# A graph layer's own-row messages: from one per row tile, closed by an identity product, to one per four tiles, transposed, added to the copied sums

## The chip, the cores and the metric

The kernel runs on one core of one Trainium2 chip. The metric is the device time of one execution in microseconds. The core has five engines that run their own instruction queues in order: TensorE (PE; its weight loads are listed as PEld), VectorE (DVE), ScalarE (ACT), GpSimd (POOL) and SyncE (SP, which here issues the transfers). They wait for each other through semaphores.

## The reference, cut to what matters

Four graph layers follow each other on 2708 rows of 128 features. The adjacency matrix `adj` is 2708 by 2708, symmetric in its pattern, with under one per cent of its entries set and every diagonal entry set. The change is in layer 1:

```python
h = maximum(layernorm(x), 0)
s = h @ msg_w[:, :D].T
d = h @ msg_w[:, D:].T
messages = gelu(s[:, None, :] + d[None, :, :] + msg_b)
aggregated = einsum('ijd,ij->id', messages, adj)
new = concatenate([h, aggregated], -1) @ upd_w.T + upd_b
x = x + layernorm(gelu(new) + h)
```

Row i receives, from every column j with adj[i, j] not zero, a message weighted by that entry. One of these columns is j = i: the message of the row to itself is gelu(h_i @ (W_s + W_d) + msg_b), weighted by adj[i, i]. That one message per row is what the change treats differently.

## The kernel before, in words

Layer 0 (to about 215 us) reads the adjacency matrix once, forms layer 0's product with it, writes a transposed copy, and lists for each row, in 22 blocks of 124 columns, up to eight entries per block (`val`, `col`). The diagonal entries are taken out of these lists and kept in `own`, a tile of 128 partitions by 22 row tiles (L292 fills it).

Layer 1 (about 215 to 615 us) works on 22 row tiles of 128 rows (the last has 20). A prologue (L827 to L839) enters layer 0's result, normalises, transposes h into `hT`, and forms the split destination rows `d3` (three bf16 parts). Then comes one period for each row tile, `period(t)`, L709, with steps k = 0 to 5. The order of all instructions on every engine is that of this hand-written sequence: the whole stretch stands under a manual schedule (L826). In one period:

- `combine(t, k)` (L602) adds, by one-hot bf16 products on TensorE, source and destination rows of four blocks into the PSUM tile `p_m`, which has two buffers; `activate(t, k)` (L621) takes the Gelu on ScalarE into `g`.
- `gather(t, k)` (L627), two steps later, multiplies `g` with `put` (the weights at their rows) in fp32 and adds into `agg`, the transposed sums, one PSUM tile for four row tiles.
- `put` for the next tile is written partly by GpSimd (`put_values`, L530, eight instructions at the start of a period) and partly by ScalarE (`put_more`, L540).
- For later tiles, at the same time: `pass_on` (L548), `fetch` (L485), `rank` (L459), `describe` (L465), `select_rows` (L472), `columns` (L562), `place` (L499), `finish_rows` (L481). The last four are VectorE's. The product of `fetch` reads the tile `sel` that `finish_rows` wrote at step 4 of the period before.
- Every even period calls `sources(k)` (L570) at step 2 for the next pair of tiles: a product with 256 columns (L580: 128 for the source part, 128 for the sum of both weight halves, `src_self`), one VectorE addition out of PSUM (L587), the split of the source half into three bf16 parts (`split`, L416), and for the other half a Gelu (L596) and two scalings by `own` (L599) on ScalarE. The result `gs` is the weighted message of each row to itself.
- `close_tile(t - 1)` (L639) at step 1 adds `gs` to the sums through a product with the identity (L645), and after the last tile of a group of four copies the sums to SBUF (`aggT`, L649 to L654).
- `update(g, step)` (L660) works on a finished group in eight steps over eight periods. Step 0 falls into period 4g+5: the product `p_u` (L671, L672), which reads `aggT`.

PSUM tiles with the tag "r" share one buffer (the pool of L405 has one): `p_r` of `rank`, `p_w` of `pass_on`, `p_s` of `sources` and `p_u` of `update` are written one after the other, each after the last reader of the one before.

Layers 2 and 3 (from about 615 us) begin with transfers of the transposed matrix (`a<-adjT`, L1082), which write memory that layer 1 has used; their first one waits for the last product of layer 1 (L672).

Of the kernel before, what the change touches and what calls it, by code (L numbers as in the profile page):

```python
# [20 lines left out]
F32 = mybir.dt.float32  # L21
BF16 = mybir.dt.bfloat16
AF = mybir.ActivationFunctionType
# [7 lines left out]
P = 128  # L31
N = 2708
D = 128
# [27 lines left out]
def listed_layers(ctx: ExitStack, tc: tile.TileContext, x, adj, w, out, flag):  # L61
# [85 lines left out]
    def span(t, k):  # L147

        return t * P, min(k * P, N - t * P)
# [245 lines left out]
    with (  # L395
# [11 lines left out]
        msg_wT, upd_wT = load(fix, "msg_wT"), load(fix, "upd_wT")  # L407
        upd_b, ln_w, ln_b = load_rows(fix, "upd_b"), load_rows(fix, "ln_w"), load_rows(fix, "ln_b")
        msg_b = load_rows(fix, "msg_b")

        src_self = fix.tile([P, 2, D], F32, name="src_self")
        nc.vector.tensor_copy(src_self[:, 0, :], msg_wT[:, 0, :])
        nc.vector.tensor_tensor(src_self[:, 1, :], msg_wT[:, 0, :], msg_wT[:, 1, :], ALU.add)

        d3 = fix.tile([P, NB, 3, D], BF16, name="d3")
        def split(dst, src, rest):  # L416

            nc.scalar.copy(dst[0], src)
            nc.vector.tensor_tensor(rest, src, dst[0], ALU.subtract)
            nc.scalar.copy(dst[1], rest)  # L420
            nc.gpsimd.tensor_tensor(dst[2], rest, dst[1], ALU.subtract)
# [145 lines left out]

        own_rows, aggs = {}, {}

        def sources(k):  # L570

            p = rpool.tile([P, CH], F32, tag="r", name="p_s")
            pv = p.rearrange("p (t c d) -> p t c d", t=2, c=2)
            sb = once.tile([P, 2, 2, D], F32, name="sb")
            m = size(2 * k + 1)
            if m < P:
                nc.vector.memset(sb[:, 1, :, :], 0.0)
            for q in range(2):
                c, mq = (2 * k + q) * P, size(2 * k + q)
                nc.tensor.matmul(  # L580
                    p[0:mq, q * 2 * D : (q + 1) * 2 * D], hT[:, c : c + mq],
                    src_self.rearrange("p c d -> p (c d)"), start=True, stop=True,
                )
            bv = msg_b.unsqueeze(1).to_broadcast([P, 2, D])
            if m == P:
                bv = msg_b.unsqueeze(1).unsqueeze(1).to_broadcast([P, 2, 2, D])
                nc.vector.tensor_tensor(sb, pv, bv, ALU.add)  # L587
            else:
                for q in range(2):
                    mq = size(2 * k + q)  # L590
                    nc.vector.tensor_tensor(sb[0:mq, q, :, :], pv[0:mq, q, :, :], bv[0:mq, :, :], ALU.add)
            s3 = three.tile([P, 3, 2, D], BF16, name="s3")
            rest = once.tile([P, 2, D], F32, name="s_r")
            split([s3[:, q, :, :] for q in range(3)], sb[:, :, 0, :], rest)
            gs = three.tile([P, 2, D], F32, name="gs")
            nc.scalar.activation(gs, sb[:, :, 1, :], AF.Gelu)  # L596
            for q in range(2):
                t = 2 * k + q
                nc.scalar.activation(gs[:, q, :], gs[:, q, :], AF.Identity, scale=own[:, t : t + 1])  # L599
            own_rows[k] = s3, gs  # L600

        def combine(t, k):  # L602

            st = state[t]
            s3 = own_rows[t // 2][0]
            b0 = 4 * k
            n = min(4, NB - b0)
            p = mpool.tile([P, 4, D], F32, name="p_m")
            for b in range(b0, b0 + n):
                kb = width(b)  # L610
                for q in range(3):
                    nc.tensor.matmul(  # L612
                        p[:, b - b0, :], st["sel"][:, b, :], s3[:, q, t % 2, :], start=(q == 0), stop=False
                    )
                for q in range(3):
                    nc.tensor.matmul(  # L616
                        p[:, b - b0, :], st["cols"][0:kb, b, :], d3[0:kb, b, q, :], start=False, stop=(q == 2)
                    )
            st["p", k] = p
# [7 lines left out]
        def gather(t, k):  # L627

            st = state[t]
            m = size(t)  # L630
            if k == 0 and t % 4 == 0:
                aggs[t // 4] = acc.tile([P, 4, P], F32, name="agg1")
            agg = aggs[t // 4][:, t % 4, 0:m]
            g = st.pop(("g", k))
            for b in range(4 * k, min(4 * k + 4, NB)):
                put = (st["put", 0][:, b, 0:m] if b < HP else st["put", 1][:, b - HP, 0:m])
                nc.tensor.matmul(agg, g[:, b - 4 * k, :], put, start=(b == 0), stop=False)  # L637

        def close_tile(t):  # L639

            state.pop(t)
            m = size(t)
            g = t // 4
            gs = own_rows[t // 2][1]
            nc.tensor.matmul(aggs[g][:, t % 4, 0:m], gs[0:m, t % 2, :], ident[0:m, 0:m], start=False, stop=True)  # L645
            first, k = GROUPS[g]
            if t == first + k - 1:
                p = aggs[g]
                aggs[g] = once.tile([D, 4, P], F32, name="aggT")  # L649
                if m < P:  # L650
                    nc.scalar.copy(aggs[g][:, 0 : k - 1, :], p[:, 0 : k - 1, :])
                    nc.scalar.copy(aggs[g][:, k - 1, 0:m], p[:, k - 1, 0:m])
                else:
                    nc.scalar.copy(aggs[g][:, 0:k, :], p[:, 0:k, :])  # L654


        STEPS = 8
# [51 lines left out]
        def period(t, between=()):  # L709
# [5 lines left out]
            for k in range(GB):  # L715
# [17 lines left out]
                    fetch(t + 2, k - 1)  # L733
                if k == 1 and a:
                    describe(t + 3)
                if k == 2:
                    if now and t % 2 == 0 and t + 2 < NT:
                        sources(t // 2 + 1)
                    if a:
                        select_rows(t + 3)  # L740
                    if now and t + 4 < NT:
                        count_rows(t + 4)
                    updates(t)
# [64 lines left out]

        def split_destinations(g):

            rest = once.tile([P, 4, D], F32, tag="sb", name="d_r")
            for src, dst, q0, q1, k in state.pop(("d", g)):
                r = rest[0:k, q0:q1, :]
                nc.vector.tensor_tensor(r, src, dst[0], ALU.subtract)
                nc.scalar.copy(dst[1], r)
                nc.gpsimd.tensor_tensor(dst[2], r, dst[1], ALU.subtract)
# [9 lines left out]
        with tc.manual_schedule():  # L826
            for step, n in (  # L827
# [877 lines left out]
```

## Time and profile before

| | |
|---|---|
| median of three runs | 1073.51 us (1072.81 to 1073.60) |
| span of the profiled execution (first to last instruction) | 1069.6 us |
| outside that span, taken against the median | 3.9 us |
| layer 1's loop, 280 to 615 us: PE, DVE, ACT, POOL busy | 323.7, 249.6, 214.7, 208.2 us of 335 |
| layer 1's prologue, 215 to 280 us: PE, DVE, ACT, POOL busy | 30.0, 47.8, 28.4, 20.9 us of 65 |
| granted TensorE clock in the prologue and in the loop | 0.62 and 1.00 |

The profile lists no separate total time for the profiled execution; its span of 1069.6 us is what the working below is made against, and the rest of 3.9 us is taken as unchanged. A row of the profile's groups reads: line, engine, operation, output<-input, shape, count, busy time in us, mean ns of one, then the idle time just before it and what ended that. A matmul in fp32 is listed as two records. Durations of matmuls overlap (they are pipelined), so what one costs is read from the distance of starts, not from its duration.

### The profile page before, as it was taken

How to read it: one execution, taken by the hardware profiler on the slowest of the kernel's cores; microseconds unless marked ns; L12 is line 12 of the kernel's file. 1: busy time of each engine (PE TensorE's matmuls, PEld its weight loads, DVE VectorE, ACT ScalarE, POOL GpSimd, SP SyncE). 2: the span in 40 equal slices, each digit the busy share in tenths (PEclk: the TensorE clock that was granted, in tenths of full speed). 3: DMA queues.
4: the chain of work that ended last, by engine and by line, in shares of the span. 5: the costliest groups of instructions: out<-in, count | busy, mean ns of one | idle time of the engine just before them, and what ended most of it. 6: DMA issues, size and time to landing. Idle time of an engine off the chain costs nothing. (4 is left out here: it accounts for less than half of the span.)

```text
span 1069.6 us, 21992 instructions
## 1 busy us (share of the span) xinstructions
PE 950.0 (89%) x7950; PEld 754.1 (71%) x7950; DVE 824.4 (77%) x2853; ACT 515.4 (48%) x1428; POOL 398.7 (37%) x476
## 2 busy tenths in 40 slices
PE   5798889934799999999999979999978999999993
PEld 2454445433799999899899934444578999999772
DVE  7999999768577798787878265666578977997673
ACT  7777777634766666666666522433321200320142
POOL 3311112022776656666766163343410300430132
PEclk9999999766799999999999979999989999999996
DMA  9888996221233433322221075566300000000000
GB/s 365 315 303 316 316 342 243 78 65 46 88 109 106 124 95 106 106 91 83 97 96 57 28 256 186 185 225 216 91 22 26 9 1 1 6 15 1 2 15 14
DMA packets 60625, 129.67 MB, mean 121 GB/s; under 512 B 11160, under 2 KB 23828, under 8 KB 57798
## 3 DMA queue, kind: packets, MB, share of 16 engines
q1 hardware_dynamic: 58690, 125.38, 34.2%
q10 hardware_dynamic: 1816, 2.80, 0.8%
q8 instruction: 64, 1.05, 0.4%
q14 instruction: 55, 0.45, 0.1%
HBM read 81.55 MB, written 30.87 MB: 105 GB/s over the span
## 5 line engine op out<-in xcount | busy, mean ns | idle before, releaser
L955 PE MATMUL att<-hv,wt 128*128 128x129 f32 (+2 forms) x1936 | 243.8, 283 | 8.7 <-DVE wt L923 8.7
L955 PEld LDWEIGHTS att<-hv,wt 128*128 128x128 f32 (+2 forms) x1936 | 224.7, 192 | 25.8 <-DVE wt L923 10.1
L923 DVE SCALAR_TENSOR_TENSOR wt<-row,lift,mask 128x1024 f32<-128x1024 f32 (+5 forms) x176 | 160.3, 939 | 34.9 <-PE att L955 34.8
L536 POOL TENSOR_SCALAR put<-mine,value 128x128 f32<-128x128 bf16 x176 | 149.8, 867 | 70.3 <-DVE mine L433 67.9
L612 PE MATMUL p_m<-s,sel 128*128 128x128 bf16 x1452 | 161.6, 220 | 5.4 <-ACT g L624 5.4
L616 PE MATMUL p_m<-d,cols 124*128 124x128 bf16 (+1 forms) x1452 | 161.7, 220 | 1.4 <-DVE cols L566 1.3
L121 POOL TENSOR_TENSOR n_r<-n_r,minus_half 128x4 f32<-128x4 f32 (+1 forms) x31 | 46.1, 1486 | 286.5 <-DVE n_r L120 280.9
L637 PE MATMUL agg<-put,g 128*128 128x128 f32 (+1 forms) x968 | 135.9, 281 | 0.0
L297 PE MATMUL acc<-a,hs 128*128 128x512 f32 (+2 forms) x264 | 124.4, 574 | 10.8 <-ACT hs L137 10.8
L309 PEld LDWEIGHTS p_T<-ident,a 128*128 128x128 f32 x484 | 60.1, 144 | 88.3 <-issue 40.3
L637 PEld LDWEIGHTS agg<-put,g 128*128 128x128 f32 x968 | 118.2, 192 | 0.0
L1094 PE MATMUL p_agg<-a,hs 128*128 128x512 f32 (+2 forms) x264 | 109.3, 556 | 7.3 <-DMA a<-adjT 7.2
L612 PEld LDWEIGHTS <-sel 128*128 128x128 bf16 x1452 | 104.3, 98 | 10.8 <-issue 7.0
L285 DVE FIND_INDEX8 col<-val,a 128x8 uint16<-128x124 f32 (+1 forms) x400 | 108.1, 285 | 0.0
L309 PE MATMUL p_T<-ident,a 128*128 128x128 f32 x484 | 82.3, 289 | 26.2 <-ACT aT L313 19.4
L624 ACT ACTIVATE g<-p_m 128x512 f32<-128x512 f32 x132 | 73.1, 554 | 63.8 <-PE p_m L616 63.8
L616 PEld LDWEIGHTS <-cols 124*128 124x128 bf16 (+1 forms) x1452 | 102.5, 98 | 1.9 <-DVE cols L566 1.9
L544 ACT ACTIVATE put<-mine,value 128x128 f32<-128x128 bf16 x308 | 100.5, 391 | 0.0
L283 DVE MAX8 val<-a 128x8 f32<-128x124 f32 (+1 forms) x400 | 92.8, 276 | 2.5 <-DMA a<-in_adj 2.5
L313 ACT ACTIVATE aT<-p_T 128x512 f32<-128x512 f32 (+2 forms) x132 | 71.1, 541 | 47.9 <-ACT aT L313 32.7
L1094 PEld LDWEIGHTS p_agg<-a,hs 128*128 128x128 f32 (+1 forms) x264 | 47.5, 194 | 55.8 <-issue 54.2
L297 PEld LDWEIGHTS acc<-a,hs 128*128 128x128 f32 (+1 forms) x264 | 44.7, 202 | 25.9 <-issue 14.8
(252 smaller groups left out, 1418.7 us busy)
## 6 DMA issues: line engine op xcount, KB each, us to landing
a<-in_adj SPq DMA_DIRECT2D x21, 1354.0 KB
adjT<-aT SPq DMA_DIRECT2D x105, 256.0 KB
a<-adjT SPq DMA_DIRECT2D x20, 1280.0 KB
spread<-passed SPq DMA_DIRECT2D x22, 704.0 KB
later<-sel SPq DMA_DIRECT2D x22, 616.0 KB
row<-own_d ACTq DMA_DIRECT2D x10, 256.0 KB
later<-sel SPq DMA_DIRECT2D x22, 82.5 KB
adjT<-aT SPq DMA_DIRECT2D x21, 74.0 KB
```

Source lines behind the costliest of these rows:

```text
L283: nc.vector.max(val[:, n, b, :], block(b))
L285: nc.vector.max_index(col[:, n, b, :], val[:, n, b, :], block(b))
L297: nc.tensor.matmul(accs[ci][:, 0:cw], h[0:m, n, :], sets[n // 4][0:m, n % 4, c : c + cw], start=(n == 0), stop=(n == NT - 1),)
L309: nc.tensor.transpose(p[0:k, q * P : q * P + m], sets[gi][0:m, q, j * P : j * P + k], ident[0:m, 0:m])
L536: nc.gpsimd.tensor_scalar(st["put", 0][:, b, :], st["mine"][:, b, :], st["value"][:, b : b + 1], None, ALU.mult)
L544: nc.scalar.activation(st["put", 1][:, b - HP, :], st["mine"][:, b, :], AF.Identity, scale=st["value"][:, b : b + 1])
L612: nc.tensor.matmul(p[:, b - b0, :], st["sel"][:, b, :], s3[:, q, t % 2, :], start=(q == 0), stop=False)
L616: nc.tensor.matmul(p[:, b - b0, :], st["cols"][0:kb, b, :], d3[0:kb, b, q, :], start=False, stop=(q == 2))
L637: nc.tensor.matmul(agg, g[:, b - 4 * k, :], put, start=(b == 0), stop=False)
L923: nc.vector.scalar_tensor_tensor(wt[0:kj, :], row[0:kj, k, c : c + n], lift[0:kj, j, k : k + 1], mask[0:kj, j, c : c + n], op0=ALU.max, op ...
L955: nc.tensor.matmul(banks[s // 3][0:m, s % 3, :], wt[0:kj, q * P : q * P + m], hv[0:kj, j, k, :], start=(v < 2 and s // 3 not in touched), ...
L1094: nc.tensor.matmul(pa[:, 0:n], h[0:k, j, :], a[0:k, j - j0, 0:n], start=(j == 0), stop=(j == NT - 1))
```

## The change

`sources` no longer forms the own message: its product has 128 columns, the VectorE addition 256 elements, and the Gelu and the two scalings are gone. In their place, for each group of four row tiles:

- `self_messages(g)`, step 2 of period 4g+1: one product of `w_self` (the sum of the weight halves) with 512 columns of `hT`, into a new PSUM tile `p_self` of the tag "r"; a Gelu with the bias column `msg_b1` on ScalarE into `gs`, transposed and with one buffer.
- `load_own(g)`, step 2 of period 4g: a transfer that spreads the group's diagonal entries to all partitions (`own_b`). They come from `own_dram`, written in the prologue by `turn_own` (a transposition on TensorE, a ScalarE copy, a transfer).
- `weigh_selfs(g)`, last step of period 4g+1: GpSimd multiplies `gs` by `own_b`.
- In `close_tile`, after the copy to `aggT`, GpSimd adds `gs` to it; the identity product is gone.

`w_self` is formed by GpSimd; VectorE's two instructions for `src_self` are gone. `split_destinations` keeps its scratch under another tag.

```diff
@@ layer 1, weights
+        msg_b1 = fix.tile([P, 1], F32, name="msg_b1")
+        nc.sync.dma_start(msg_b1, w["msg_b"].rearrange("(k p) -> p k", p=P), allow_slow_non_contiguous=True)
-        src_self = fix.tile([P, 2, D], F32, name="src_self")
-        nc.vector.tensor_copy(src_self[:, 0, :], msg_wT[:, 0, :])
-        nc.vector.tensor_tensor(src_self[:, 1, :], msg_wT[:, 0, :], msg_wT[:, 1, :], ALU.add)
+        w_self = fix.tile([P, D], F32, name="w_self")
+        nc.gpsimd.tensor_tensor(w_self, msg_wT[:, 0, :], msg_wT[:, 1, :], ALU.add)
@@ new functions
+        own_dram = dram.tile([NT, P], F32, name="own_dram")
+        def turn_own(_):
+            p = rpool.tile([P, CH], F32, tag="r", name="p_own")
+            nc.tensor.transpose(p[0:NT, 0:P], own, ident)
+            turned = once.tile([NT, P], F32, name="own_T1")
+            nc.scalar.copy(turned, p[0:NT, 0:P])
+            nc.sync.dma_start(own_dram, turned)
+        def load_own(g):
+            t, k = GROUPS[g]
+            n = span(t, k)[1]
+            own_cols[g] = once.tile([P, CH], F32, name="own_b")
+            nc.sync.dma_start(
+                own_cols[g][:, 0:n],
+                own_dram[t : t + k, :].rearrange("t i -> (t i)")[0:n].partition_broadcast(P),
+            )
+        def self_messages(g):
+            c, n = span(*GROUPS[g])
+            p = rpool.tile([P, CH], F32, tag="r", name="p_self")
+            nc.tensor.matmul(p[:, 0:n], w_self, hT[:, c : c + n], start=True, stop=True)
+            selfs[g] = once.tile([D, CH], F32, name="gs")
+            nc.scalar.activation(selfs[g][:, 0:n], p[:, 0:n], AF.Gelu, bias=msg_b1)
+        def weigh_selfs(g):
+            n = span(*GROUPS[g])[1]
+            nc.gpsimd.tensor_tensor(selfs[g][:, 0:n], selfs[g][:, 0:n], own_cols.pop(g)[:, 0:n], ALU.mult)
@@ sources
-            sb = once.tile([P, 2, 2, D], F32, name="sb")
+            sb = once.tile([P, 2, D], F32, name="sb")
-                nc.tensor.matmul(
-                    p[0:mq, q * 2 * D : (q + 1) * 2 * D], hT[:, c : c + mq],
-                    src_self.rearrange("p c d -> p (c d)"), start=True, stop=True,
-                )
+                nc.tensor.matmul(pv[0:mq, q, :], hT[:, c : c + mq], msg_wT[:, 0, :], start=True, stop=True)
-                nc.vector.tensor_tensor(sb, pv, bv, ALU.add)
+                nc.vector.tensor_tensor(sb, pv, msg_b.unsqueeze(1).to_broadcast([P, 2, D]), ALU.add)
-            gs = three.tile([P, 2, D], F32, name="gs")
-            nc.scalar.activation(gs, sb[:, :, 1, :], AF.Gelu)
-            for q in range(2):
-                t = 2 * k + q
-                nc.scalar.activation(gs[:, q, :], gs[:, q, :], AF.Identity, scale=own[:, t : t + 1])
@@ gather, close_tile
-                nc.tensor.matmul(agg, g[:, b - 4 * k, :], put, start=(b == 0), stop=False)
+                nc.tensor.matmul(agg, g[:, b - 4 * k, :], put, start=(b == 0), stop=(b == NB - 1))
-            nc.tensor.matmul(aggs[g][:, t % 4, 0:m], gs[0:m, t % 2, :], ident[0:m, 0:m], start=False, stop=True)
+                n = span(first, k)[1]
+                flat = aggs[g].rearrange("d t i -> d (t i)")[:, 0:n]
+                nc.gpsimd.tensor_tensor(flat, flat, selfs.pop(g)[:, 0:n], ALU.add)
@@ period
+                if k == 2 and now and t % 4 == 1:
+                    self_messages(t // 4)
+                if k == GB - 1 and now and t % 4 == 1:
+                    weigh_selfs(t // 4)
+                if k == 2 and now and t % 4 == 0:
+                    load_own(t // 4)
                 if k == 2:
                     if now and t % 2 == 0 and t + 2 < NT:
                         sources(t // 2 + 1)
@@ split_destinations
-            rest = once.tile([P, 4, D], F32, tag="sb", name="d_r")
+            rest = once.tile([P, 4, D], F32, tag="aggT", name="d_r")
@@ prologue
-                (place, 0), (pass_on, 0), (sources, 0), (enter, 3), (spread_sums, 4), (split_destinations, 1),
+                (place, 0), (pass_on, 0), (turn_own, 0), (sources, 0), (enter, 3), (spread_sums, 4), (split_destinations, 1),
```

More of the change, by code (lines that the diff above doesn't have):

```diff
@@ L570, in sources @@
+        own_cols, selfs = {}, {}
         def sources(k):
             p = rpool.tile([P, CH], F32, tag="r", name="p_s")
-            pv = p.rearrange("p (t c d) -> p t c d", t=2, c=2)
-            sb = once.tile([P, 2, 2, D], F32, name="sb")
+            pv = p[:, 0 : 2 * D].rearrange("p (t d) -> p t d", t=2)
+            sb = once.tile([P, 2, D], F32, name="sb")
             m = size(2 * k + 1)
             if m < P:
-                nc.vector.memset(sb[:, 1, :, :], 0.0)
+                nc.vector.memset(sb[:, 1, :], 0.0)
@@ L578, in sources @@
             for q in range(2):
                 c, mq = (2 * k + q) * P, size(2 * k + q)
-                nc.tensor.matmul(
-                    p[0:mq, q * 2 * D : (q + 1) * 2 * D], hT[:, c : c + mq],
-                    src_self.rearrange("p c d -> p (c d)"), start=True, stop=True,
-                )
-            bv = msg_b.unsqueeze(1).to_broadcast([P, 2, D])
+                nc.tensor.matmul(pv[0:mq, q, :], hT[:, c : c + mq], msg_wT[:, 0, :], start=True, stop=True)
             if m == P:
-                bv = msg_b.unsqueeze(1).unsqueeze(1).to_broadcast([P, 2, 2, D])
-                nc.vector.tensor_tensor(sb, pv, bv, ALU.add)
+                nc.vector.tensor_tensor(sb, pv, msg_b.unsqueeze(1).to_broadcast([P, 2, D]), ALU.add)
@@ L590, in sources @@
                     mq = size(2 * k + q)
-                    nc.vector.tensor_tensor(sb[0:mq, q, :, :], pv[0:mq, q, :, :], bv[0:mq, :, :], ALU.add)
+                    nc.vector.tensor_tensor(sb[0:mq, q, :], pv[0:mq, q, :], msg_b[0:mq, :], ALU.add)
             s3 = three.tile([P, 3, 2, D], BF16, name="s3")
             rest = once.tile([P, 2, D], F32, name="s_r")
-            split([s3[:, q, :, :] for q in range(3)], sb[:, :, 0, :], rest)
-            gs = three.tile([P, 2, D], F32, name="gs")
-            nc.scalar.activation(gs, sb[:, :, 1, :], AF.Gelu)
-            for q in range(2):
-                t = 2 * k + q
-                nc.scalar.activation(gs[:, q, :], gs[:, q, :], AF.Identity, scale=own[:, t : t + 1])
-            own_rows[k] = s3, gs
+            split([s3[:, q, :, :] for q in range(3)], sb, rest)
+            own_rows[k] = s3
         def combine(t, k):
             st = state[t]
-            s3 = own_rows[t // 2][0]
+            s3 = own_rows[t // 2]
             b0 = 4 * k
@@ L643, in close_tile @@
             g = t // 4
-            gs = own_rows[t // 2][1]
-            nc.tensor.matmul(aggs[g][:, t % 4, 0:m], gs[0:m, t % 2, :], ident[0:m, 0:m], start=False, stop=True)
             first, k = GROUPS[g]
```

## The prediction

> **What bounds the kernel now.** First the page: busy shares and slices.
>
> ```profile
> PE 950.0 (89%) x7950; PEld 754.1 (71%) x7950; DVE 824.4 (77%) x2853; ACT 515.4 (48%) x1428; POOL 398.7 (37%) x476
> ...
> PE   5798889934799999999999979999978999999993
> ...
> PEclk9999999766799999999999979999989999999996
> ```
>
> TensorE is the fullest engine; in layer 1's loop (slices 11 to 22, 280 to 615 us) it is at 90% or more. So I asked what ends its idle time there, 285 to 600 us:
>
> ```profile
> PE p_m L612 <- ACT g L624: 5.4, 7, 1.4
> PE y L493 <- DVE sel L483: 3.0, 4, 0.9
> PE p_m L616 <- DVE cols L566: 1.3, 2, 0.6
> ```
>
> Only 9.7 us: work taken from TensorE's queue moves the loop's end, except where ScalarE or VectorE comes last. The seven ScalarE waits all lie in even periods, those with `sources`. ScalarE in period 12:
>
> ```profile
> 467.76 0.41 ACT L420 CAST s<-s_r 128x256 bf16<-128x256 f32 x1 [0.49 <-DVE s_r L419]
> 468.08 0.41 ACT L596 ACTIVATE gs<-sb 128x256 f32<-128x256 f32 x1
> 468.52 0.69 ACT L599 ACTIVATE gs<-gs,own 128x128 f32<-128x128 f32 x2
> 469.12 1.63 ACT L137 ACTIVATE hs<-xs,n_r 128x128 f32<-128x128 f32 x4
> 470.66 0.97 ACT L544 ACTIVATE put<-mine,value 128x128 f32<-128x128 bf16 x3
> 471.53 0.57 ACT L624 ACTIVATE g<-p_m 128x512 f32<-128x512 f32 x1
> ```
>
> From here ScalarE runs without a gap until the Gelu whose end releases TensorE at 472.16 (wait 1.45). The two `gs` rows, 468.08 to 469.12, are 1.04 us of that chain, and the change removes them. Third, TensorE at step 2 of period 9, where the new product will stand:
>
> ```profile
> 416.94 1.11 PE L637 MATMUL agg<-put,g 128*128 128x128 f32 x8
> 417.89 0.44 PE L493 MATMUL y<-xb,sel 128*128 128x37 bf16 x11
> 418.17 0.47 PE L671 MATMUL p_u<-upd_wT,hT 128*128 128x128 f32 x2
> ```
>
> Starts matter, not durations: eight fp32 records take 0.945 us (416.94 to 417.89), 0.118 each. Last, ScalarE at the loop's start:
>
> ```profile
> 280.31 0.41 ACT L807 CAST d<-p_d 124x128 bf16<-124x128 f32 x2
> 280.63 0.59 ACT L624 ACTIVATE g<-p_m 128x512 f32<-128x512 f32 x1
> 281.11 0.24 ACT L554 COPY where_T<-p_w 22x128 bf16<-22x128 bf16 x1
> 281.38 0.31 SPq L556 DMA_DIRECT2D passed<-where_T  x1
> 281.40 0.17 PE L461 MATMUL p_r<-rows_n,before 128*128 128x22 bf16 x1 [1.32 <-ACT where_T L554]
> ```
>
> ScalarE is gapless and TensorE waits 1.32 us for it.
>
> **What the Trainium skill says.** "Perfetto Trace Analysis", Optimizing Tensor Performance: independent matmul groups should rotate through different PSUM banks, so that the evacuation of one overlaps the next. The tag "r" has one bank; the 1.32 us above is such a wait, so the trace agrees. "ScalarE: Activation LUTs", What ACT_TABLE_LOAD costs: 1283 ns and a drain of 1380. The trace has the load at 249.91 for 1283 ns and the Gelu at 251.21; I see no drain and use 1.3 us. "SBUF — State Buffer", Who interferes with whom: VectorE instructions in two-port modes or with two SBUF inputs contend with GpSimd. The trace agrees: L427 takes 231 to 726 ns, L536 593 to 2387.
>
> **The change part by part** (negative is gain, us).
>
> (a) Identity products, 22: in full periods start to next start is 0.30 (339.72 to 340.02), without `p_r` ahead 0.23 (600.63 to 600.86). 22 x 0.27 = -5.9.
>
> (b) `sources`: four records of 256 columns take 0.95 (313.89 to 314.84); half the columns, like L637, 4 x 0.118 = 0.47. Ten calls in the loop: -4.7. VectorE's addition goes from 691 ns to 414 (the 256-element form, L591), so VectorE, which waits for `p_s`, is released 0.47 + 0.28 = 0.75 earlier.
>
> (c) `p_self`: 512 columns in two records; 256 columns take 0.237 a record, so 0.95. Five whole groups and one of 148 columns (0.27): +5.0.
>
> (d) A new wait. In TensorE's order of the changed kernel `p_u` of group g stands directly after `p_self` of group g+1, in the same bank, and its first product waits for the Gelu of `p_self`. From the last record's slot end to ScalarE's start is 0.26 (L616 to L624, 360.97 to 361.23); the Gelu with a bias column costs 0.687 (L1117, same shape), release 0.05: 1.0. Queued behind `p_u` on TensorE is everything, step 3's `combine` first; VectorE's L676 waits too, so both shift together and nothing hides it. Periods 5, 9, 13, 17: 1.0; period 21, 148 columns (383 ns): 0.7. Sum +4.7. Bounds: 0.8, if the hand-overs take a quarter of that, to 1.5, if ScalarE is still on its Gelu of step 2 when `p_self` ends; before, in period 9, it was free from 418.61, half a microsecond ahead of `p_self`'s end at 419.1, so I take the middle. Period 1 has no `p_u`.
>
> (e) ScalarE's relief: 1.04 + 0.28 = 1.32 after `p_s` ends. Of the seven waits, 0.81, 0.43, 0.43, 1.45, 0.43, 1.45, 0.38, only 0.13 stays of each long one: -5.1. What is late next is `sel`. VectorE comes only 0.75 earlier after `p_s`, TensorE 0.47 + wait + 0.27 per close. Each tile's `sel` must be done on VectorE before `y` at step 1 of the next period reads it; where it ends close before, TensorE's surplus comes back as a wait for `sel`. Worked for each even period from `p_s` to that `y`. Period 0: 0.47 + 0.81 + 0.27 = 1.55 against 0.75 and a slack of 0.44: 0.36 comes back. Periods 10 and 14: no slack (`y` already waits 0.8), and VectorE has no gap through the next period either, up to its wait for `p_s` in period 12, so two closes count: TensorE would gain 0.47 + 0.43 + 0.54 = 1.44, VectorE 0.75, so 0.69 each. Period 18: 0.47 + 0.38 + 0.27 less 0.75, 0.37. Periods 12 and 16: slack 0.96 (`sel` ends at 477.57, `y` starts at 478.53); 0.47 + 1.32 + 0.27 = 2.06 against 0.75 + 0.96 = 1.71: 0.35 each. In periods 2, 4, 6 and 8 the two gains are equal or the slack covers the rest. Sum +2.8; bounds 0 and the whole 5.1.
>
> (f) Table load: the first Gelu is now `activate(0, 0)`, so in ScalarE's order the load moves from 249.91, where ScalarE soon waits for VectorE anyway (0.57 at 252.92), to just ahead of 280.63, where nothing hides it: `where_T` behind it comes 1.3 later, and with it `p_r` and all that TensorE has queued: +1.3. Bounds 0 (if it could run in an earlier gap) and 2.7 (with the drain that the page states).
>
> (g) Prologue: VectorE loses two instructions (220.00 to 220.32) and 0.28 of L587, in stages that follow it: -0.55. `turn_own` puts a transposition (estimated 0.4 at this clock, a record of L155) and a copy (0.25, as L554) with hand-overs of 0.3 ahead of `p_s`, +0.95, while `p_s` there falls from 1.87 (245.70 to 247.57) to half, -0.9. Net -0.5. `w_self` fits GpSimd's idle time (17.4 before 221.97). SP: `msg_b1`'s issue (0.43, as L104) ends by 220, the next is at 223.44; `own_dram`'s stands behind `spread`, and 24 us before the next `later`.
>
> (h) GpSimd: six multiplications and six additions, 1.27 each (L692) to 2.54 beside VectorE. It waits 67.9 us in 17 waits for `mine`, about 4 a period; where it has none (427.12) `put` is used a period later, so delay there is hidden by some 14 us. `xb` is ready 6 us ahead. Without that cover 12 x 1.3 = 15 would show. VectorE held by an addition: bounds 0 and 1.27 each; I take 0.5 (L427's spread) in periods 12 and 16, which (e) leaves without slack: +1.0. `own_b` (SP issue about 0.35) follows `spread` on SP, long before `later` needs the queue: 0; if `later` came late by its transfer, at most 1 in five periods.
>
> (i) Tail: GpSimd's addition on 148 columns (estimated 0.5: 0.54 for 176 in L421) stands between copy and L672, whose end releases SP's first `a<-adjT` (614.94), for which TensorE then waits 6.1: +0.45. Layers 2 and 3: unchanged.
>
> Sum: -5.9 - 4.7 + 5.0 + 4.7 - 5.1 + 2.8 + 1.3 - 0.5 + 1.0 + 0.45 = -0.95. The span of 1069.6 becomes 1068.65; with the 3.9 outside it (median 1073.51 less the span, taken as unchanged), 1072.6.
>
> **The rivals.** Forecast: gains and the new wait nearly cancel. 0.2% of the median is 2.1 us, about what a measurement of this kernel can tell from no change: within 1071.4 to 1075.6.
>
> Faster: ScalarE's relief is kept. If VectorE's chain is no limit, neither the 2.8 of (e) nor the 1.0 of (h) comes: -4.75, 1068.8. For it: VectorE is busy 249.6 of the loop's 335 us. Against: `sel` already ends four waits, three of 0.8 to 0.9.
>
> Slower: contention on the shared SBUF port. The ten large GpSimd operations of (h), in periods 4g at steps 1 to 2 and 4g+1 at step 5, could each hold VectorE for their own 1.27, 12.7 in all; half of that, 6.4, on the sum without contention (-1.95) gives +4.4: 1077.9. It decides from 0.4 us per operation, 4.1 in all, which is what lifts the sum over +2.1. For it: L427's spread. Against: periods 4g have slack at `p_s` (VectorE waits 2.3 to 2.6 there), and GpSimd's `put`, eight instructions a period, has run beside VectorE all along without `sel` being last in most periods.
>
> That the own message isn't moved at all is excluded: the order of instructions shows it.
>
> **How the numbers follow.** Forecast 0.42, faster 0.36, slower 0.22: these are the chances of the three outcomes too. The likeliest case's own range is 1071.4 to 1075.6. The 80% range runs from 1068 (relief kept, waits of (d) at 0.8) to 1077.5, leaving out the slower rival's upper part.
>
> **What would show it.** After: no L645; `p_u` waiting for ACT `gs` five times, about 1 us each; `g` waits of TensorE near zero, `sel` waits from 3.0 to about 6; the table load before 282; `aggT` released by POOL at the end. Wrong would be: `p_u` waits of 2 us, `p_r` without the extra 1.3, VectorE instructions longer beside GpSimd's 128x512 ones.

## The result, and the profile after

The changed kernel takes 1080.3 us (median of 11 runs, 1076.0 to 1084.8); the kernel before, on the same chip, 1073.3 us (11 runs, 1069.0 to 1076.4). The ratio is 1.0065 with a 95% interval of 1.0046 to 1.0084: slower by 5 to 9 us. Measured again beside later experiments it was 1.0084 (1.0066 to 1.0102). The forecast of 1072.6 us lies below both; the range up to 1077.5 missed it too.

The profiled execution of the changed kernel took 1078.44 us, its span 1076.6 us, so 1.84 us lie outside the span. (The table above took 3.9 us for the kernel before, by comparing its span with a median of other executions. That was no measurement: its profiled execution was about 2 us faster than the median.) All that follows compares spans and parts of spans of profiled executions; medians judge whole kernels.

Lines after, in the order of those shown of before. The page: TensorE is busy 3.0 us less, and no slice of these rows tells where 7 us more came from; a slice is 27 us long.

```profile
PE 947.0 (88%) x7919; PEld 749.3 (70%) x7919; DVE 831.4 (77%) x2851; ACT 508.8 (47%) x1402; POOL 409.4 (38%) x489
...
PE   5798888944899999989899969999978999999993
...
PEclk9999999756899999999999979999999999999996
```

TensorE's waits in 285 to 600 us (line, waited for, sum, times, longest):

```profile
PE y L494 <- DVE sel L484: 6.0, 9, 1.1
PE p_u L697 <- ACT gs L596: 3.4, 4, 0.8
PE p_m L637 <- ACT g L649: 3.3, 2, 2.0
PE p_m L641 <- DVE cols L567: 3.1, 4, 1.1
```

The waits for ScalarE's Gelu `g` fell from seven to two, but one of these two is longer than any before. Those for VectorE (`sel`, `cols`) doubled, from 4.3 to 9.1. The new waits of `p_u` are close to the forecast: 0.84 each, besides the hand-overs. Here is one of them, on TensorE in period 9:

```profile
417.32 1.10 PE L594 MATMUL p_self<-hT,w_self 128*128 128x512 f32 x2
419.26 0.49 PE L697 MATMUL p_u<-upd_wT,hT 128*128 128x128 f32 x2 [0.84 <-ACT gs L596]
```

ScalarE in period 12, where the two `gs` rows stood that are gone:

```profile
466.43 0.41 ACT L419 CAST s<-sb 128x256 bf16<-128x256 f32 x1 [0.75 <-DVE sb L617]
468.47 0.41 ACT L421 CAST s<-s_r 128x256 bf16<-128x256 f32 x1 [1.64 <-DVE s_r L420]
468.78 1.65 ACT L137 ACTIVATE hs<-xs,n_r 128x128 f32<-128x128 f32 x4
...
471.21 0.57 ACT L649 ACTIVATE g<-p_m 128x512 f32<-128x512 f32 x1
```

Before, ScalarE waited 0.49 for `s_r`; now 1.64. The 1.04 us of the two rows were taken up by a wait for VectorE. And the loop's start, ScalarE first, then the product behind it:

```profile
278.76 1.28 ACT L649 ACT_TABLE_LOAD   x1
280.05 0.60 ACT L649 ACTIVATE g<-p_m 128x512 f32<-128x512 f32 x1
280.55 0.24 ACT L555 COPY where_T<-p_w 22x128 bf16<-22x128 bf16 x1
280.84 0.17 PE L462 MATMUL p_r<-rows_n,before 128*128 128x22 bf16 x1 [3.29 <-ACT where_T L555]
```

The table load is where it was forecast; the wait grew from 1.32 to 3.29.

To place the 7.0 us I cut each span at the starts of `p_w`, the product of `pass_on`: p_w(t+1), for tile t+1, opens period t. The first stretch after p_w(0) holds the end of the prologue and periods 0 and 1, the next one periods 2 to 19, the last one periods 20 and 21 and layers 2 and 3. "Ratio" is that of medians; each row has one profiled execution.

| kernel | to p_w(0) | p_w(0) to p_w(3) | p_w(3) to p_w(21) | p_w(21) to end | span | median | ratio to before (95%) |
|---|---|---|---|---|---|---|---|
| before | 244.8 | 63.87 | 277.01 | 483.9 | 1069.6 | 1073.3 | 1 |
| changed | 243.3 | 66.02 | 279.95 | 487.4 | 1076.6 | 1080.3 | 1.0065 (1.0046, 1.0084) |
| d0_after_again | 243.6 | 66.18 | 279.95 | 487.0 | 1076.7 | 1079.6 | 1.0084 (1.0066, 1.0102) |
| a1_no_add | 244.0 | 66.16 | 275.66 | 487.9 | 1073.7 | 1073.9 | 1.0027 (1.0015, 1.0039) |
| a2_add_later | 245.3 | 66.15 | 278.55 | 487.8 | 1077.8 | 1079.6 | 1.0071 (1.0046, 1.0096) |
| a3_self_later | 245.7 | 63.16 | 273.45 | 487.5 | 1069.8 | 1071.6 | 0.9996 (0.9982, 1.0011) |
| a4_gelu_early | 245.0 | 64.01 | 278.78 | 489.0 | 1076.8 | 1078.2 | 1.0061 (1.0038, 1.0083) |
| c1_last_vec | 243.2 | 66.03 | 280.41 | 486.9 | 1076.5 | 1075.6 | 1.0032 (1.0019, 1.0045) |
| c2_add_vec | 243.6 | 66.15 | 276.85 | 485.9 | 1072.4 | 1073.1 | 1.0014 (1.0001, 1.0027) |
| c3_all | 244.8 | 63.03 | 275.22 | 488.2 | 1071.2 | 1069.4 | 0.9969 (0.9954, 0.9985) |
| c4_before_add | 245.9 | 63.87 | 278.24 | 483.7 | 1071.7 | 1073.5 | 1.0017 (1.0004, 1.0030) |
| d2_last_pe | 242.9 | 64.08 | 280.41 | 482.5 | 1069.9 | 1074.4 | 1.0037 (1.0024, 1.0050) |
| d1_best | 244.1 | 63.06 | 269.94 | 483.6 | 1060.6 | 1062.1 | 0.9921 (0.9902, 0.9941) |
| d3_best_late_table | 244.7 | 63.14 | 269.98 | 484.8 | 1062.7 | 1063.5 | 0.9932 (0.9911, 0.9953) |

Changed less before: -1.5, +2.15, +2.94, +3.5. The experiments look for the causes of the last three. In the kernels of a3, c3, d1 and d3 the first `p_self` stands in period 3 instead of period 1, so 0.86 moves from the second of these parts to the third.

### The profile page after: what moved, and what is told of

Same layout as the page of the kernel before. It is cut to its first block, busy times and chain, and to the rows that moved or that the text cites. A ratio compares the mean times of both kernels' runs of the same rounds, so it can differ in the third digit from the quotient of the medians.

```text
span 1076.6 us, 21961 instructions
## 1 busy us (share of the span) xinstructions
PE 947.0 (88%) x7919; PEld 749.3 (70%) x7919; DVE 831.4 (77%) x2851; ACT 508.8 (47%) x1402; POOL 409.4 (38%) x489
## 3 DMA queue, kind: packets, MB, share of 16 engines
q8 instruction: 64, 1.05, 0.4%
## 5 line engine op out<-in xcount | busy, mean ns | idle before, releaser
L537 POOL TENSOR_SCALAR put<-mine,value 128x128 f32<-128x128 bf16 x176 | 146.9, 854 | 81.8 <-DVE mine L434 76.8
L285 DVE FIND_INDEX8 col<-val,a 128x8 uint16<-128x124 f32 (+1 forms) x400 | 105.3, 271 | 0.0
L283 DVE MAX8 val<-a 128x8 f32<-128x124 f32 (+1 forms) x400 | 89.9, 261 | 2.6 <-DMA a<-in_adj 2.6
## 6 DMA issues: line engine op xcount, KB each, us to landing
adjT<-aT SPq DMA_DIRECT2D x105, 256.0 KB
row<-own_d ACTq DMA_DIRECT2D x10, 256.0 KB
```

What stands on the lines that cost most here:

```text
L283: nc.vector.max(val[:, n, b, :], block(b))
L285: nc.vector.max_index(col[:, n, b, :], val[:, n, b, :], block(b))
L537: nc.gpsimd.tensor_scalar(st["put", 0][:, b, :], st["mine"][:, b, :], st["value"][:, b : b + 1], None, ALU.mult)
```

## The experiments

Line numbers of the changed kernel: `p_self` L594, its Gelu L596, the multiplication L601, `s_r` L420, the closing addition L680, `p_u` L697 and L698. The kernel before had medians of 1071.2 to 1073.3 us beside the various kernels, so these are compared with each other by their ratios.

### a1: the additions left out

```diff
-                nc.gpsimd.tensor_tensor(flat, flat, selfs.pop(g)[:, 0:n], ALU.add)
+                if g == len(GROUPS) - 1:
+                    nc.gpsimd.tensor_tensor(flat, flat, selfs.pop(g)[:, 0:n], ALU.add)
```

> The changed kernel, but the five full groups' own messages are not added to the copied sums (that part of the result is left out; the last group's stays, so the tail is the same). Theory A, contention: in periods 8, 12, 16 and 20 the addition L680 and VectorE's subtraction s_r of `sources` start within 0.1 us of each other, and s_r takes 1.46 to 2.29 us in place of 0.42; without the addition s_r is back at 0.42 everywhere, the waits of TensorE for the Gelu g in periods 12 and 16 (1.30 and 2.02) fall to about 0.3, and the kernel is 2.5 to 4 us faster than the changed one, 3 to 4.5 us above the kernel before. Theory B, VectorE's chain up to `sel` is the limit with or without the addition: s_r is short again, but TensorE waits as much longer for `sel`, and the gain is under 1 us.

Measured: 1.0027, that is 4 to 6 us less than the changed kernel; p_w(3) to p_w(21) is 4.3 us shorter, 2.8 of it in period 16. Theory A holds for the time. The reason is seen in the trace of the changed kernel, VectorE and GpSimd together in period 12:

```profile
466.86 1.57 DVE L420 TENSOR_TENSOR s_r<-sb,s 128x256 f32<-128x256 f32 x1 [0.47 <-ACT s L419]
466.89 1.26 POOL L680 TENSOR_TENSOR aggT<-aggT,gs 128x512 f32<-128x512 f32 x1
468.12 0.72 POOL L422 TENSOR_TENSOR xb<-v_r,xb 128x176 bf16<-128x176 f32 x1
```

`s_r` takes 0.42 to 0.54 us in the other periods; here it ends 0.28 after the addition does. In periods 8, 12 and 16 it took 1.46, 1.57 and 2.29. The addition does not start when the sums are copied (399.17 in period 8) but when GpSimd has finished its eight `put` (402.75), and that falls together with `sources`.

One part of the expectation failed: `s_r` isn't back at 0.42 in a1. It takes 1.00, 0.83 and 1.07 in periods 8, 12 and 16, and the waits for `g` are 0.56 and 0.79 in place of 0.3. Period 12 of a1, VectorE and GpSimd:

```profile
466.90 0.83 DVE L420 TENSOR_TENSOR s_r<-sb,s 128x256 f32<-128x256 f32 x1 [0.47 <-ACT s L419]
466.92 0.54 POOL L422 TENSOR_TENSOR xb<-v_r,xb 128x176 bf16<-128x176 f32 x1
```

In the kernel before, `s_r` started 0.66 after this small GpSimd addition, when it was over, and took 0.43. The change brings VectorE to `s_r` earlier, and so into it. The three meetings make `s_r` 1.6 us longer in all; no run takes them away alone.

### a2: the additions two steps later

The lines of the addition move from `close_tile` into a function `add_selfs`; the last group's addition stays where it was.

```diff
+                if k == 3 and now and t % 4 == 0 and t > 0:
+                    add_selfs(t // 4 - 1)
```

> The same addition, moved from step 1 of the period after a group (where it meets s_r) to that period's step 3, where GpSimd is idle for 5.9 us and VectorE does its small n1u_r instructions and `cols`. Theory A: nearly all of the gain of leaving the addition out is kept: 2 to 4 us faster than the changed kernel, since a delay of VectorE there comes after `sources` and is covered by the waits for p_s and p_u in the next period. Theory B, or a contention that costs the same wherever the addition stands: within 1 us of the changed kernel.

Measured: 1.0071, no gain. Theory A's expectation failed, and the trace says why; period 12 again, VectorE and GpSimd:

```profile
472.67 1.26 POOL L685 TENSOR_TENSOR aggT<-aggT,gs 128x512 f32<-128x512 f32 x1
472.76 1.19 DVE L128 TENSOR_TENSOR n1u_r<-n1u_r 128x4 f32<-128x4 f32 x1
473.98 0.17 DVE L129 TENSOR_SCALAR n1u_r<-n1u_r 128x4 f32<-128x4 f32 x1
```

An instruction on four elements per partition, 0.16 us in other places, takes 1.19 and ends with the addition. So it isn't bandwidth that is shared: the later one stands still until the earlier is done. The Trainium skill says this in "SBUF — State Buffer", Who interferes with whom: a VectorE instruction with two SBUF inputs contends with a GpSimd instruction that reads SBUF, and the one that issues first keeps the shared pair for the whole instruction. The trace agrees here, where the addition starts 0.09 us ahead. (The records of the slow `s_r` and their additions start at most 0.09 apart, in period 12 with VectorE's first, so they don't tell who issued first.) The cost only moved: `s_r` is as short as in a1, but TensorE's waits for `sel` rose from 6.0 to 8.0, in periods 5, 13 and 17 by 0.4 to 1.0 each.

### a3: p_self in another step

```diff
-                if k == 2 and now and t % 4 == 1:
-                    self_messages(t // 4)
-                if k == GB - 1 and now and t % 4 == 1:
-                    weigh_selfs(t // 4)
+                whole = now and t + 1 == sum(GROUPS[t // 4])
+                if k == 3 and whole:
+                    self_messages(t // 4)
+                if k == GB - 1 and whole:
+                    weigh_selfs(t // 4)
```

> p_self and its Gelu moved from step 2 of a group's second tile, where p_u of the group before stands directly behind it in the one bank of tag r, to step 3 of its last tile, where the next to use the bank is p_w, some 7 us later. Theory A (the prediction's step d): the five waits of p_u for the Gelu, 3.9 us in all and about 4.5 with the hand-overs that no wait shows, are gone and nothing takes their place: periods 5, 9, 13 and 17 shorter by 0.9 to 1.0 each, 3.5 to 4.5 us faster than the changed kernel. Theory B: the time returns as waits for `sel` or for the Gelu g (ScalarE now has the Gelu of the own messages in step 3, ahead of put and g): under 1.5 us faster.

Measured: 0.9996, 7 to 9 us less than the changed kernel and level with the kernel before. All waits of `p_u` for the Gelu are gone. Period 5 fell from 17.37 to 15.40 us: 0.86 for `p_self`, which now costs that much in period 3, and 1.1 for the wait with its hand-overs. Four such periods make 4.4. The rest is more than was expected: 2.0 us before p_w(3) and 2.5 us in period 16, and neither place has a `p_u`. The first, and 1.6 of the second, turned out to be the clock (below).

### a4: the Gelu table earlier

```diff
+        def first_gelu(_):
+            one = fix.tile([P, 1], F32, name="one")
+            nc.scalar.activation(one, msg_b1, AF.Gelu)
-                (destinations, 2), (rows, 3), (turn_rows, 3), (finish_rows, 1), (fetch_both, 1), (enter, 4),
+                (destinations, 2), (rows, 3), (turn_rows, 3), (finish_rows, 1), (fetch_both, 1), (first_gelu, 0), (enter, 4),
```

> A Gelu of one column is added in the prologue, in a gap in which ScalarE waits 6.8 us for VectorE, so that the table of Gelu is loaded there and not just ahead of the first Gelu g of the loop. Theory A: the wait of p_r at the loop's start falls from 3.29 to about 2 (the 1.28 of the load), and since TensorE idles less there the granted clock of 281 to 285 us is back from 0.61 near 1.0, which took about another 1 us: 1.5 to 2.5 us faster than the changed kernel. Theory B: the load is worth only itself, and the clock stays low: 1.0 to 1.3 us. Theory C: TensorE's wait there is set by something else (VectorE's last d_r): under 0.5 us.

Measured: 1.0061, which by time alone can't be told from the changed kernel, so the gain of theory A isn't seen in the medians. In the trace the wait of `p_r` is 1.1 and p_w(0) to p_w(3) is 64.0 in place of 66.0, but the end of this execution was 1.6 us longer. The clock explains the 2.0; in stretches of one us each (here the changed kernel; the column before the last two is the granted clock):

```profile
281.00:282.00 1.00, 1.00 (x27) 1.00 (x24) 0.48 (x3) 0.15 (x1) 0.49 (x1) 0.94 0.03 6
282.00:283.00 1.00, 1.00 (x12) 1.00 (x11) 0.26 (x3) 1.00 (x5) 0.78 (x2) 0.50 0.07 16
...
285.00:286.00 1.00, 1.00 (x20) 0.99 (x19) 0.01 (x1) 0.29 (x2) 1.00 (x3) 0.86 0.70 241
```

From 281.9 to 285.3 TensorE ran at half clock for 3.4 us and so lost 1.7 us of work. Over all fourteen profiles the wait of `p_r` tells which kernels show it: the six with a wait of 3.24 to 3.58 us have the dip and 66.0 to 66.2 us between p_w(0) and p_w(3). The eight with 1.1 to 2.97 have none, and 63.9 to 64.1 (0.86 added where `p_self` has moved). Among these eight are kernels with the load late (d2, a3, d3) and early (a4, c3, d1), and they don't differ: without the dip the load itself costs nothing there, because with an early load TensorE waits longer for `sel` in period 1 (0.81 in d1). The Trainium skill, "TensorE: Matmul & The Clock Gate", Part 1, says that the clock is halved after an idle window of about 3.4 us and that these windows run freely. The trace agrees in the length of the dip and in its places: the changed kernel has a second dip in period 16, and the two start 256.0 us apart (281.88 and 537.88, worked out from the shares of the slices in which they begin), 75 times 3.413.

That second dip follows a wait of only 2.02 us for `g` at 536.63. Four profiles with this wait show it (changed, d0, c1, d2: period 16 lasts 18.2 us); a4 has the same wait and no dip (16.6), and c4 even 2.39 and none. So 1.6 us of period 16 are the clock's.

The clock records show what decides. In each profile all changes of the clock lie on a grid of 3.413 us, and this grid falls differently in each execution: the clock first rises between 13.8 and 17.2 us after the start. Here are three windows of these grids, with TensorE's busy time as the second figure: the one ahead of the dip of period 16 in the changed kernel, the one with most of the same wait in a4, and the one with most of the wait of 2.97 at the loop's start in d2:

```profile
534.46:537.87 3.41, 1.39 (x19) 1.24 (x17) 3.20 (x11) 3.41 (x11) 0.84 (x1) 1.00 0.55 173
534.60:538.01 3.41, 1.62 (x21) 1.61 (x21) 3.17 (x11) 3.41 (x11) 0.45 (x1) 1.00 0.65 203
278.76:282.17 3.41, 1.71 (x37) 1.71 (x36) 0.73 (x4) 2.34 (x6) 2.67 (x5) 1.00 0.01 2
```

Only the first is followed by a dip. Over all profiles, windows at full clock that start between 275 and 600 us: each of the ten dips follows one with TensorE busy for 0.12 to 0.42 of it, and all 1314 windows without a dip behind them have 0.48 or more. So a wait brings the clock down where it leaves one window mostly idle, and not where two windows share it; which of the two happens is a matter of the execution. That goes beyond the idle window of which the page speaks, and the measurement decides. It holds for this loop: at its end, behind products with 20 columns, the clock also falls after windows that count as fully busy (609.28 to 612.69 in the kernel before).

### c1: the last group's addition on VectorE

```diff
                 agg = aggs.pop(g)
+                if g == len(GROUPS) - 1:
+                    n = span(t, k)[1]
+                    flat = agg.rearrange("d t i -> d (t i)")[:, 0:n]
+                    nc.vector.tensor_tensor(flat, flat, selfs.pop(g)[:, 0:n], ALU.add)
```

> The changed kernel with only the last group's addition (148 columns) taken from GpSimd and made by VectorE just ahead of that group's p_u. Theory A, a queue blocked at its head: at the end of layer 1 GpSimd waits 5.3 us at this addition for the copied sums, and the power n_r (L121) of group 4's second normalization, which is ready 3.3 us earlier, stands behind it in GpSimd's order; VectorE waits 4.4 us for that power, and all that follows, up to the last hs and the masks whose release lets layer 2's transfers start, is late. From the last p_w to the end, 483.9 us before and 487.4 to 489.0 in the changed kernel and three variants, should go back to 484 to 485: 2.5 to 3.5 us faster than the changed kernel. Theory B: the longer end is only the addition itself and the spread between runs: 0 to 0.7 us.

Measured: 1.0032 by time, 3.5 to 5.5 us better than the changed kernel, but the profiled execution shows only 0.5 us at the end (486.9): inconclusive as a test of the cause. GpSimd's power is indeed no longer late, and the last `hs` of layer 1 starts where it did before the change (under d2), but now VectorE's order is the obstacle: `p_u` of the last group waits 3.3 us, since VectorE makes the addition at 620.87, behind all of group 4's second step, and layer 2's first transfer, released by that `p_u`, starts at 623.12 in place of 619.56.

### c2: all additions on VectorE, just ahead of p_u

```diff
                 agg = aggs.pop(g)
+                n = span(t, k)[1]
+                flat = agg.rearrange("d t i -> d (t i)")[:, 0:n]
+                nc.vector.tensor_tensor(flat, flat, selfs.pop(g)[:, 0:n], ALU.add)
```

> All six additions made by VectorE just ahead of p_u, where it waits 3.1 us for p_u; none on GpSimd. Theory A: the contention (4.0 us when the additions were left out) and the blocked queue at the end (about 3 us) are both gone, and VectorE's own 0.69 us per group lies in a wait: 6 to 8 us faster than the changed kernel, within 1.5 us of the kernel before. Theory B: VectorE's chain up to `sel` is the limit in these periods too, and five additions of 0.69 come back as waits for `sel` or later p_u: 3 to 4.5 us faster than the changed kernel only.

Measured: 1.0014, 5.5 to 7.5 us better than the changed kernel. Most of the contention is gone (p_w(3) to p_w(21) 276.85 against 275.66 without additions), but the 1.2 us between them show that VectorE's 0.69 isn't quite hidden: the waits of `p_u` grew from 0.8 to between 1.05 and 1.29, since the Gelu ahead of `p_u` writes the one buffer of `gs`, which VectorE's addition must have read.

### c3: three repairs together

a3, a4 and c2 in one kernel.

> Additions on VectorE ahead of p_u, p_self at step 3 of the group's last tile, and an early Gelu for the table: all three repairs together. If they are separate causes, the sum from the measured parts is -7 (additions) -7 (p_self, of which 4.5 are its waits and the rest came from the clock at the loop's start and from period 16, which the other repairs may already have) -1.3 (table): 10 to 14 us faster than the changed kernel, 3 to 7 us faster than the kernel before. Rival: VectorE's chain up to `sel` is then the limit, the repairs overlap, and the kernel ends within 2 us of the kernel before.

Measured: 0.9969, faster than before by 1.6 to 5 us. The repairs add up only in part. TensorE still waits 4.3 us for VectorE's additions ahead of `p_u` in four periods and 3.6 at the end, for the reason seen in c1.

### c4: only an addition, in the kernel before

```diff
                     nc.scalar.copy(aggs[g][:, 0:k, :], p[:, 0:k, :])
+                    nc.gpsimd.tensor_tensor(aggs[g][:, 0:k, :], aggs[g][:, 0:k, :], aggs[g][:, 0:k, :], ALU.add)
```

> The kernel before, with nothing of the change but a GpSimd addition of 512 columns after the copy of each full group's sums (the sums are added to themselves, so their values are doubled there). It measures the contention alone. Theory A: s_r of `sources` in periods 8, 12, 16 and 20 is held by about 1 to 1.9 us as in the changed kernel, and there ScalarE's chain to the Gelu that TensorE waits for (1.45 in periods 12 and 16) is longer by as much: 2 to 4.5 us slower than the kernel before. Theory B: the addition hurts only in the changed kernel, whose VectorE has lost slack: under 1 us.

Measured: 1.0017 (0.4 to 3.2 us), between the two theories. The trace has `s_r` at 0.67 in period 12 and 1.37 in period 16, and p_w(3) to p_w(21) grew by 1.2. The addition meets `s_r` only in part here, because VectorE comes to it at another moment. The price of such a pair is set by the overlap, up to the whole GpSimd instruction, and the overlap by timing that the change itself shifts.

### d0: the changed kernel once more

> The changed kernel itself, once more, as the measure for the others of this call. 1.0065 [1.0046, 1.0084] times the kernel before was measured first; the same within that interval is expected, and from the last p_w of layer 1 to the end about 487 us again (483.9 in the kernel before).

Measured: 1.0084, with the same parts within 0.4 us.

### d2: only the last group's own messages, by TensorE

```diff
+            if g == len(GROUPS) - 1:
+                q = t - first
+                nc.tensor.matmul(aggs[g][:, q, 0:m], ident, selfs[g][:, q * P : q * P + m], start=False, stop=True)
-                nc.gpsimd.tensor_tensor(flat, flat, selfs.pop(g)[:, 0:n], ALU.add)
+                if g < len(GROUPS) - 1:
+                    nc.gpsimd.tensor_tensor(flat, flat, selfs.pop(g)[:, 0:n], ALU.add)
@@ period: p_self of the last group at step 3 of period 20
```

> The changed kernel with only the last group's own messages taken off GpSimd: they are added by two identity products on TensorE; for that their p_self stands one tile earlier, at step 3. Theory A, GpSimd's queue blocked at its head by the last addition: from the last p_w to the end falls from about 487.4 to 484 to 484.5 us, and the kernel is 2.5 to 3.5 us faster than the changed one (0.5 of it from p_u's wait in period 21, which goes too). Theory B, that time was spread between runs: it stays at 487 and the gain is 0.5.

Measured: 1.0037, 5 us better than the changed kernel measured beside it (d0; about 2.7 to 7.4 by the two intervals), and p_w(21) to the end is 482.5 in place of 487.0 to 487.4. Theory A holds in its direction; its size is taken apart below. GpSimd in the changed kernel:

```profile
611.37 0.50 POOL L601 TENSOR_TENSOR gs<-gs,own_b 128x148 f32<-128x148 f32 x1
617.18 0.50 POOL L680 TENSOR_TENSOR aggT<-aggT,gs 128x148 f32<-128x148 f32 x1 [5.31 <-issue]
617.63 1.04 POOL L121 TENSOR_TENSOR n_r<-n_r,minus_half 128x4 f32<-128x4 f32 x1
```

and in d2:

```profile
607.76 1.26 POOL L722 TENSOR_TENSOR u<-u,ln_b 128x512 f32<-128x512 f32 x1
611.75 1.04 POOL L121 TENSOR_TENSOR n_r<-n_r,minus_half 128x4 f32<-128x4 f32 x1 [2.73 <-DVE n_r L120]
```

The power `n_r` belongs to group 4, has its input at 614.3 in the changed kernel, and runs at 617.63, because the addition ahead of it in GpSimd's order waits for the last tile's sums. VectorE waits 4.36 us for it, and the last `hs` starts 55.3 us after p_w(21), where it was 53.0 before the change. In d2 and in c1 it is back at 52.9, and in a3, which at this place only takes away `p_u`'s wait in period 21, it is 0.7 earlier than in the changed kernel. So the blocked order costs at most 2.3 us here, and 1.6 if the 0.7 add to it.

The rest of the 4.5 to 4.9 us that d2 gains lies in layers 2 and 3, which the change doesn't touch. From the last `hs` to layer 2's first `p_rz` it is 8.8 to 9.0 us in the kernel before, c4 and d1, and 10.2 to 10.7 in the changed kernel, d0, d2 and d3: these have a dip of the clock in between. And after p_w(21) this execution of d2, the fastest of its 16, had 34.1 us at half clock (without the last slow stretch of each execution), the two of the changed kernel 44.4 and 37.5. That part can't be put down to GpSimd's order.

### d1 and d3: every part in the place that the runs point to

`add_selfs` is VectorE's here and stands right behind `describe`, whose `v_r` is the last thing that VectorE does before it waits for `p_s`. `p_self` is placed as in a3 (the last group's in period 20), the last group's messages as in d2, and d1 has the early Gelu of a4, d3 has not.

```diff
+                if k == 1 and now and t % 4 == 0 and t > 0:
+                    add_selfs(t // 4 - 1)
```

> All repairs in the places that the earlier runs point to: p_self at step 3 of a group's last tile; the five full groups' additions on VectorE right behind v_r in the period after the group, where it otherwise waits 2.0 us for p_s; the last group's own messages added by two identity products on TensorE, as in the kernel before, so that no addition stands in GpSimd's or VectorE's order at the end of layer 1; the Gelu table loaded early. Against the kernel with the additions just ahead of p_u (3.0 to 4.4 us faster than before by its chain of waits less 4.3 us in four waits of p_u for VectorE's addition and 3.6 in one at the end): 4 to 8 us faster than that one, 6 to 10 us faster than the kernel before. Rival: the waits for `sel` (5.6 us) take up what the p_u waits gave, and it is within 2 us of that kernel.

> As the kernel with all repairs, but the Gelu table is loaded where the change puts it, at the loop's start. Theory A: 1.3 us slower than with the early table, the load itself, and up to 3 us where TensorE's longer wait there lets its granted clock fall for some 4 us. Theory B: under 0.5 us.

Measured: d1 0.9921 (0.9902 to 0.9941), 6.3 to 10.5 us faster than before and some 17 faster than the change as made; d3, with the late table, 0.9932. The difference of d1 and d3 (1.4 us of medians) is within their intervals. Neither has a dip at the loop's start, and up to p_w(3) the late load costs them nothing that shows (63.06 and 63.14). TensorE's waits in d1, 285 to 594 us:

```profile
PE y L494 <- DVE sel L484: 5.2, 6, 1.1
PE p_m L641 <- DVE cols L567: 2.3, 3, 0.9
PE p_m L637 <- ACT g L649: 1.2, 3, 0.5
```

No wait of `p_u` is left, and those for ScalarE are down to 1.2. What still ends TensorE's idle time is VectorE's chain.

## Why the prediction was wrong, by its own steps

The prediction's terms, put on the same cuts: +0.6 up to p_w(3), -2.1 from there to p_w(21), +0.6 after, -0.95 in all. Measured: -1.5 ahead of p_w(0), +2.15 from there to p_w(3), +2.94 and +3.5.

- (a), (b), (c): right in size. Even periods without other events got 0.79 shorter (forecast 0.74), odd ones 0.2 to 0.3 (0.27), and `p_self` costs 0.86 (0.95). In periods 11, 15 and 19 the 0.27 of (a) came back at once: `y` waits 1.13 for `sel` in place of 0.8 to 0.9.
- (d), the wait of `p_u`: right, 1.06 in periods 5 and 17 (1.0), with 0.84 of it shown as a wait.
- (e), give-back: named rightly, mis-sized. Where no addition disturbs (a1), the waits for `g` fell by 4.0 (forecast 5.1), those for `sel` rose by 2.6 (forecast 2.8), but those for `cols`, another VectorE instruction that the step didn't follow, rose by 1.6 too. The step also took VectorE's earlier release as pure gain, while it brought `s_r` into GpSimd's small addition (a1).
- (f), the table load: the place was right, the mechanism of its price wrong. "+1.3" for the load itself was not what was paid; 2.0 was, by the clock that the longer wait of TensorE brought down. Three kernels with the late load (a3, d2, d3) didn't pay it: their waits of 2.67 to 2.97 fell across two windows of the clock's grid. This term looked at what is queued, and not at what an idle TensorE does to the next 3.4 us.
- (h), contention: the step that failed in the loop. It took 0.5 in two periods, 1.0 in all. The additions cost 4.3 between p_w(3) and p_w(21), by a1: 2.8 in period 16 (1.6 of it the second dip), 0.7 each in periods 8 and 12, 0.5 in period 13, less 0.4 that comes back in period 17. The rival "slower" had this mechanism and its threshold of 0.4 per operation; the four additions of these periods cost 1.07 on average, 0.68 without the dip. I argued it down by the slack of VectorE at `p_s`. But the addition waits for GpSimd's `put` to end, and starts when that slack is over; and `put` beside VectorE was no model for it, since a VectorE instruction meets it by chance, not each time. What the six multiplications (L601) cost was not tried.
- (i), the tail: the step that failed at the end. "+0.45" counted the addition on the path of the sums to `p_u`. What stands behind the waiting addition on GpSimd, a normalization of the group before, was not looked up. With it and `p_u`'s wait the last `hs` came 2.3 us later. A dip of the clock behind that `hs` took another 1.2 to 1.7; d2 and d3 have it without the blocked order, so whether the change brings it stays open. The same question was asked of TensorE in (d), and rightly answered there.
- (g) and what lies ahead: p_w(0) came 1.5 earlier than before, although nearly all that precedes it is unchanged. Over the kernels it varies between 242.9 and 245.9, so I take the 1.5 as spread between executions; no run tests it. The 3.9 outside the span was wrong, as said: with 1.84 the same sum would have given 1070.5.

The misses by place, against the 8.0 between -0.95 and the +7.1 that the four parts sum to: the additions 3.3 (4.3 less 1.0, with 1.6 of clock in them), the loop's start 1.6, the end 2.9, less 1.5 ahead of p_w(0). The remaining 1.7, in periods 2 to 19, is of the size of what (e) missed (`cols` 1.6, `g` 1.1); it was not separated by a run of its own. Of what the clock took, 2.0 and 1.6 in the loop and 1.2 to 1.7 behind it, nothing was in the prediction.

## What to carry to other kernels

Every instruction that a change adds must be asked the same three questions on every engine, the idle one above all: what does it wait for, what stands behind it in that engine's order, and which instruction of another engine does it meet when it at last starts. A GpSimd operation that reads SBUF cost a VectorE instruction with two SBUF inputs up to its whole length where the two met, so it belongs where VectorE waits anyway, or on VectorE itself at that place; here that choice, a PSUM bank's next user moved by a step, and an end left to TensorE turned +0.65% to -0.8%. And a wait of TensorE of 2 to 3 us isn't priced at its length: look at the granted clock of the 5 us after it, and take a dip, or its absence, in one execution as that execution's own.

## What the runs showed that was not expected

- A VectorE instruction on 128x4 elements took 1.19 us in place of 0.16 beside a GpSimd addition of 1.26: it stood still until the other ended.
- A dip of the granted clock to 0.50 lasted 3.4 us, began about when TensorE resumed work (0.05 us before to 1.24 after), and cost 1.6 to 2.0 us in the loop. Waits of 3.24 to 3.58 us had it 6 times of 6, those of 2.02 us in period 16 4 times of 5, those of 1.1 to 2.97 at the loop's start not once in 8. What told them apart was the busy share of one window of 3.413 us: 0.42 and less with a dip, 0.48 and more without.
- Taking the additions away did not give `s_r` back its 0.42 us: released earlier, it met another GpSimd instruction and took 0.83 to 1.07.
- The table load of 1.28 us was followed by its Gelu at once (278.76 + 1.28 = 280.04, start at 280.05), and its price vanished in another wait.
